# Masked graph attention on one core: forming W_v's first difference by a negation and an adding transfer, and issuing the loads of q from GpSimd

## The chip, the core and the metric

The kernel runs on one core of a Trainium2 chip. The core has five engines with queues of their own: TensorE (PE, matrix products, with its weight loads shown apart as PEld), VectorE (DVE), ScalarE (ACT), GpSimd (POOL) and SyncE (SP, which only issues transfers). Transfers between device memory and on-chip memory run on 16 DMA engines, whoever issues them. The metric is the device time of one execution in microseconds; the median of the runs counts, lower is better. The profile is one further execution, taken by the hardware profiler.

## What is computed

One layer of attention over a sparse random graph of 2708 nodes with 1024 features, all in float32:

```python
h = jnp.maximum(_layernorm(x, axis=-1), 0.0)
q = h @ W_q.T + b_q
k = h @ W_k.T + b_k
v = h @ W_v.T + b_v
z = (q @ k.T) / sqrt(1024)
z = z * adj
z = jnp.where(z == 0.0, -10000.0, z)
out = softmax(z, axis=1) @ v
x = x + jnp.maximum(out, 0.0)
```

A node has few neighbours (an entry of adj is one with probability 0.0014771), so only the scores of real neighbours matter.

## The kernel before

**Stages.** The kernel first finds the neighbours of every node, normalizes the rows to h, and sorts the nodes by their number of neighbours into tiles of 128. It folds W_q and W_k into one matrix M, so that a tile's scores are products of a row of q' = hM + b with gathered rows of h. It then runs through *units*, each a pair of tiles. Units 0 to 9 (the q units) multiply tiles of h by M and store q' rows to device memory (`q_dram` for tiles 0 to 7, `q_late` for 8 and up). Units 10 and up (the output units) multiply the attention's weighted sums u by W_v, apply the relu, add x and scatter the rows to the output. One last tile, `alone`, follows the pairs.

**Products in seven blocks.** A unit's product of a 2x2 blocked pair of tiles with a 2x2 blocked matrix is computed with seven block products instead of eight (a scheme of Strassen's kind). The matrix enters as its four blocks, held in the tile `M` (slots `M[:,0,0]`, `M[:,0,1]`, `M[:,1,0]`, `M[:,1,1]`), and as four differences, held in `T`, a view of the tile `wlow` (the name that the profile shows). Each block is 128 x 2048 in float32, 1 MB. `opened(n+1)` starts a unit during the one before it: first a11 times `M[:,0,0]`, then s1 times `T[:,0]`. `multiply` goes through the remaining five blocks and calls `after(0)` to `after(6)` between them; what a step of the neighbourhood attention or a load does "at (n, i)" is issued there.

**Change of matrix.** When the last q unit (unit 9) runs, `M` and `T` pass from the folded matrix to W_v, block by block, as TensorE finishes with them. SP loads b12, b11, b22 and b21 (line 1266; b22 twice, once into `T[:,1]`), and VectorE forms the four differences (line 1270): T0 = b12 - b11, T1 = b22 - T0, T2 = b22 - b12, T3 = b21 - T1.

**Attention beside the units.** `attention` is a stream of steps that VectorE works off between the blocks. For a tile t, `fetch` loads its q' rows into one of two buffers (`pq`, pool tag `hT`): tiles below 8 by a gather from `q_dram` issued by GpSimd, later tiles by a plain load from `q_late` issued by SP (line 833). The tile of overflow entries (`SECOND`) has half of its rows from each (line 831). `fill` gathers neighbours' rows of h into free slots (line 610, tiles `g`); there are eleven slots, and two more once `M[:,0,1]` is free for good, at (10, 1). VectorE computes the scores (line 863, gathered row times q' row), ScalarE the exponentials and the first weighted row (line 912), VectorE the sum of the rest (line 923). A slot comes free when its row has been added. Finished sums go to `u_dram`, and SP loads them back as rows `or` for the output units, by quarters for VectorE's transposes (line 705) or whole.

**Order.** VectorE's instructions stand in the order in which the program writes them. For TensorE, ScalarE, GpSimd and SP a scheduler sets the order from unit 4 on, by its own estimate of when things are ready; each engine then goes through its instructions in that order, and an instruction that waits holds up those behind it on its engine. The lines that the change touches are in `fetch` (828 to 836), `opened` (1025), `after` (1262 to 1272) and the end for `alone` (1373).

Of the kernel before, what the change touches and what calls it, by code (L numbers as in the profile page):

```python
# [14 lines left out]
AF = mybir.ActivationFunctionType  # L15
ALU = mybir.AluOpType
AX = mybir.AxisListType

P = 128
# [10 lines left out]
EARLY = 8  # L30
# [35 lines left out]
def tile_preln_masked_attention(  # L66
# [12 lines left out]
    nc = tc.nc  # L79
# [3 lines left out]
    scale = 1.0 / math.sqrt(D)  # L83
# [11 lines left out]
    HP = P // 2  # L95
# [16 lines left out]
    q_late = dram.tile([(BARE - EARLY) * P, D], FT, name="q_late")  # L112
# [63 lines left out]
    t = 0  # L176
    while t < NT:
# [4 lines left out]
        t = e  # L182
# [17 lines left out]
    M = core.tile([P, 2, 2, 4, NB], FT, name="M")  # L200
# [232 lines left out]
    T = wlow.rearrange("p (k a) (b w) -> p k (a b) w", a=2, b=2)  # L433
# [12 lines left out]
    with tc.tile_pool(name="w", bufs=1, side="left") as wp:  # L446
# [11 lines left out]
        t1 = [work.tile([P, D], FT, tag="hT", name=f"t1_{k}", bufs=2) for k in range(2)]  # L458
# [61 lines left out]
        if True:  # L520
# [13 lines left out]
            for o in range(DC):  # L534
# [4 lines left out]
                else:  # L539
                    k = o - H  # L540
# [18 lines left out]
        Z = [psum.tile([P, NB], FT, tag="acc", name=f"ps_z{i}") for i in range(H)]  # L559
# [47 lines left out]
    def gather(dst, src, t, w, n, skip=False):  # L607
        off = bass.IndirectOffsetOnAxis(ap=ptab.bitcast(U32)[:n, t, w:w + 1], axis=0)
        if skip:
            return nc.gpsimd.indirect_dma_start(out=dst, out_offset=None, in_=src, in_offset=off,  # L610
                                                bounds_check=N - 1, oob_is_err=False)
        return nc.gpsimd.indirect_dma_start(out=dst, out_offset=None, in_=src, in_offset=off)
# [176 lines left out]
    slots, free = [], []  # L789
# [13 lines left out]
    wanted, g_of, tq, first_q = [], {}, {}, []  # L803
# [11 lines left out]
    def ask(t):  # L815

        g_of[t] = []
        wanted.extend((t, s) for s in range(K[t]))

    def fetch(t):  # L820

        if t not in g_of:
            ask(t)
        if t == BARE:
            return
        assert formed.issuperset(range(EARLY) if t < EARLY or t == SECOND else (t,)), t
        tq[t] = work.tile([P, D], FT, tag="hT", name=f"pq_{t}", bufs=2)
        if t == SECOND:
            assert EARLY in formed
            gather(tq[t][:HP], q_dram[:, :], t, SLOTS - WIDE, HP)  # L830
            nc.sync.dma_start(tq[t][HP:], q_late[:HP, :])
        elif t >= EARLY:
            nc.sync.dma_start(tq[t], q_late[(t - EARLY) * P:(t - EARLY + 1) * P, :])
        else:
            got = gather(tq[t], q_dram[:, :], t, SLOTS, P)
            if t == order[0]:
                first_q.append(got)
# [171 lines left out]
    def add_block(bank, a, b, last=True):  # L1009
        for c in range(4):  # L1010
            mm = nc.tensor.matmul(bank, a[:, c, :], b[:, c, :], start=False, stop=(c == 3), skip_group_check=True)  # L1011
        return mm
# [3 lines left out]
    def opened(n):  # L1016

        if n not in banks_of:
            return
        X, Z = banks_of[n]  # L1020
        ops = ops_of[n][0]
        add_block(X, ops["a11"], M[:, 0, 0])
        Y = psum.tile([P, NB], FT, tag="acc", name="psy")
        nc.scalar.copy(Y, X)
        products.append(add_block(Z, ops["s1"], T[:, 0]))
        p5 = small("p5")
        nc.scalar.copy(p5, Z)
        opened_of[n] = Y, p5
# [158 lines left out]
    def of_wv(i, j):  # L1187

        return wv[j][:, i * 4:(i + 1) * 4, :]
# [5 lines left out]
    units = [("q",) + p for p in q_pairs] + [("o",) + p for p in o_pairs]  # L1195
# [19 lines left out]
    products = []  # L1215
    last_q = len(q_pairs) - 1
# [13 lines left out]
    for n, unit in enumerate(units):  # L1230
# [13 lines left out]
        def after(i):  # L1244
# [13 lines left out]
            if n == FIRST and i in (1, 4, 5):  # L1258
                for g in slots[:4] if i == 1 else slots[4:6] if i == 4 else slots[6:8]:
                    with tc.issue_after(sorted_at[-1].ins):  # L1260
                        nc.vector.memset(g, 0.0)
            b11, b12, b21, b22 = M[:, 0, 0], M[:, 0, 1], M[:, 1, 0], M[:, 1, 1]
            for at, place, src in (((-1, 0), b12, of_wv(0, 1)), ((0, 0), b11, of_wv(0, 0)), ((0, 2), T[:, 1], of_wv(1, 1)),
                                   ((0, 3), b21, of_wv(1, 0)), ((0, 4), b22, of_wv(1, 1))):
                if (n - last_q, i) == at:
                    nc.sync.dma_start(place, src)
            for at, place, a, b in (((0, 2), T[:, 0], b12, b11), ((0, 4), T[:, 1], T[:, 1], T[:, 0]),
                                    ((1, 0), T[:, 2], b22, b12), ((1, 1), T[:, 3], b21, T[:, 1])):
                if (n - last_q, i) == at:
                    nc.vector.tensor_sub(place, a, b)  # L1270
            if (n - last_q, i) == (1, 1):
                free.extend(M.rearrange("p i j (a c) w -> p i j a (c w)", a=2)[:, 0, 1, a, :] for a in range(2))
            if (n, i) == (FIRST, 5):
                next(stream)
            if (n, i) == (FIRST, 6):
# [39 lines left out]
            if nxt is None and i == 1:  # L1315
                uT = work.tile([P, D], FT, tag="hT", name="T_alone", bufs=2).rearrange("p (c q) -> p c q", q=P)
# [53 lines left out]
    y = work.tile([P, D], FT, tag="q", name="y_alone", bufs=4)  # L1370
    send(gather(y, x, alone, SLOTS, P))
    uT, (X, Z), p1 = single["turned"], single["banks"], single["first"]
    add_block(Z, uT[:, 0:4, :], T[:, 0])
    add_block(Z, uT[:, 4:8, :], M[:, 1, 1])
    nc.vector.tensor_add(p1, Z, p1)
    nc.vector.scalar_tensor_tensor(y[:, hi], p1, 0.0, y[:, hi], op0=ALU.max, op1=ALU.add)
# [9 lines left out]
    with tc.If(some > 0):  # L1386
# [19 lines left out]
        with tc.tile_pool(name="big", bufs=1, side="right") as big, tc.tile_pool(  # L1406
# [25 lines left out]
            for t, (t0, n) in enumerate(tiles):  # L1432
                ht = gen.tile([P, D], FT, tag="ht", name="g_h")
                nc.sync.dma_start(ht[:n], h_dram[t0:t0 + n, :])
                for s in range(DC // 4):
                    pt = psum.tile([P, 4, P], FT, tag="tp", name="g_pt")
                    for c in range(4):
                        k = s * 4 + c
                        nc.tensor.transpose(pt[:, c, :n], ht[:n, k * P:(k + 1) * P], ident[:n, :n])
                    nc.vector.tensor_copy(hT[:, s * 4:(s + 1) * 4, t0:t0 + n], pt[:, :, :n])  # L1440
            with tc.For_i(0, NT) as i:
# [9 lines left out]
                q = gen.tile([P, D + 1], FT, tag="q", name="g_q")  # L1451
# [25 lines left out]
                for b0 in range(0, N, NB):  # L1477
                    w = min(NB, N - b0)
# [84 lines left out]
```

## Time and profile before

| | |
|---|---|
| median of 3 runs | 638.18 us (637.52 to 638.37) |
| profiled execution | 638.0 us |
| its span, first to last instruction | 636.3 us |
| granted TensorE clock, mean | 0.995 |
| TensorE / VectorE / GpSimd / ScalarE busy | 98% / 83% / 57% / 45% |
| DMA | 180.11 MB, mean 283 GB/s |

The page of the profile groups instructions by line, engine and operation. A row of the timeline has the start in us from the span's start, the length in us, the engine, the line, the operation, the tiles it writes and reads, and in brackets how long its engine sat idle before it and for whom. The chain of work that ended last is followed back from the last instruction, at each step to what released it. A wait for several things is put down to the last of them. POOL rows of transfers are the time to issue them, not the transfer itself; a matmul's end is modelled.

### The profile page before, as it was taken

The numbers are of one execution on the slowest core, as the hardware profiler recorded it, in microseconds if no ns is written. First come the engines' busy times: TensorE is split into PE (matmuls) and PEld (weight loads), VectorE is DVE, ScalarE is ACT, GpSimd is POOL, SyncE is SP. The second block draws the span as 40 slices with busy tenths as digits, with TensorE's granted clock in tenths as the row PEclk, the third lists the DMA queues.
The fourth block names the chain that finished last, engine by engine and source line by source line (L and its number), as shares of the span: only waits on it lengthen the run. The fifth ranks groups of instructions, "written<-read, shape, count | busy, mean of one in ns | idle before, by whom it ended". The sixth has DMA issues, their size and how long they took to land.

```text
span 636.3 us, 6139 instructions
## 1 busy us (share of the span) xinstructions
PE 624.6 (98%) x1627; PEld 315.5 (50%) x1627; DVE 525.7 (83%) x1021; ACT 283.5 (45%) x421; POOL 361.8 (57%) x383
## 2 busy tenths in 40 slices
PE   9999999999999999999999999999999999999994
PEld 5777766444444544444444434444444444444441
DVE  5999889897995755997889999999999989898341
ACT  3539975859667533424341243443343333422300
POOL 2649960975868277563742563576566777632431
PEclk9999999999999999999999999999999999999997
DMA  8998897598696439986699998999999999893761
GB/s 339 407 372 310 334 351 298 199 342 328 246 382 221 170 113 334 326 299 196 194 289 323 297 412 216 311 318 324 351 378 321 334 299 295 242 289 95 210 217 40
DMA packets 62352, 180.11 MB, mean 283 GB/s; under 512 B 10039, under 2 KB 17031, under 8 KB 61672
## 3 DMA queue, kind: packets, MB, share of 16 engines
q0 software_dynamic: 25136, 78.41, 39.4%
q1 hardware_dynamic: 31242, 80.19, 35.8%
q10 hardware_dynamic: 5934, 21.06, 8.5%
q8 instruction: 15, 0.25, 0.2%
q14 instruction: 25, 0.20, 0.1%
HBM read 147.23 MB, written 42.31 MB: 298 GB/s over the span
## 4 chain that ended last, share of the span: by engine, by line
PE 85%; DVE 6%; issue 4%; DMA 3%; SPq 1%; POOL 0%; ACT 0%; POOLq 0%; DVEq 0%; ACTq 0%
PE ps L1011 38%; PE psy L1011 28%; PE ps_y L476 6%; PE ps_x L476 4%; PE ps_z L476 4%; PE pt L415 3%; DVE u L923 2%; DMA g<-h_dram,tab 1%; DMA or<-u_dram 1%; DVE junk L863 1%; DVE s L722 1%; DVE wlow L1270 1%; PE ps_y L511 1%; SPq L700 1%; DVE q L1092 0%
## 5 line engine op out<-in xcount | busy, mean ns | idle before, releaser
L610 POOL DMA_INDIRECT g<-h_dram,tab x94 | 121.4, 1291 | 84.4 <-DVE u L923 31.1
L1011 PE MATMUL ps<-M,a 128*128 128x512 f32 x320 | 144.0, 593 | 0.0
L1011 PE MATMUL psy<-wlow,s 128*128 128x512 f32 x320 | 143.9, 592 | 0.0
L863 DVE SCALAR_TENSOR_TENSOR junk<-g,pq 128x1024 uint8<-128x1024 f32 x93 | 113.7, 1222 | 14.0 <-DMA g<-h_dram,tab 10.9
L1011 PEld LDWEIGHTS ps<-M,a 128*128 128x128 f32 x320 | 59.8, 190 | 70.8 <-issue 70.6
L1011 PEld LDWEIGHTS psy<-wlow,s 128*128 128x128 f32 x320 | 59.7, 190 | 70.2 <-issue 69.4
L923 DVE SCALAR_TENSOR_TENSOR u<-g,coef,u 128x1024 f32<-128x1024 f32 x69 | 88.4, 1281 | 6.9 <-ACT u L912 5.8
L389 DVE FIND_INDEX8 at<-ones,adj 128x8 uint32<-128x685 f32 (+1 forms) x88 | 74.5, 865 | 0.0
L1011 PE MATMUL psy<-wlow,a 128*128 128x512 f32 x160 | 72.0, 593 | 1.4 <-DVE q L1092 1.4
L1011 PE MATMUL ps<-M,s 128*128 128x512 f32 x160 | 72.1, 592 | 0.0
L1011 PE MATMUL ps<-wlow,s 128*128 128x512 f32 x160 | 72.0, 593 | 0.1
L368 ACT ACTIVATE sized<-adj 128x2708 uint8<-128x2708 f32 (+1 forms) x22 | 54.3, 2468 | 7.5 <-DMA adj<-in_adj_dram 6.2
L298 POOL TENSOR_TENSOR hsum<-hsum,x 128x256 f32<-128x256 f32 (+1 forms) x56 | 38.7, 729 | 25.6 <-DVE wlow L444 21.2
L1110 POOL DMA_INDIRECT y<-in_x_dram,tab x19 | 34.8, 1832 | 29.1 <-ACT y L1127 15.9
L1011 PEld LDWEIGHTS psy<-wlow,a 128*128 128x128 f32 x160 | 30.3, 190 | 40.0 <-issue 37.1
L1011 PEld LDWEIGHTS ps<-wlow,s 128*128 128x128 f32 x160 | 30.3, 190 | 38.6 <-issue 37.9
L1011 PEld LDWEIGHTS ps<-M,s 128*128 128x128 f32 x160 | 30.3, 190 | 38.1 <-issue 37.4
L912 ACT ACTIVATE u<-g,coef 128x1024 f32<-128x1024 f32 x18 | 20.7, 1147 | 32.1 <-DVE coef L911 32.1
L808 POOL DMA_INDIRECT out_dram<-y,tab x21 | 25.0, 1188 | 16.4 <-DVE flag L1354 6.1
L626 POOL DMA_INDIRECT tab_dram<-tab,pos_i x22 | 21.9, 995 | 20.7 <-DVE pos_i L689 15.3
L276 ACT ACTIVATE x<-x,r 128x1024 f32<-128x1024 f32 (+1 forms) x22 | 25.9, 1235 | 7.3 <-POOL r L266 7.3
L760 ACT COPY ps<-bp_sb 128x512 f32<-128x512 f32 x42 | 24.5, 595 | 7.2 <-DVE y L1145 6.7
(251 smaller groups left out, 843.5 us busy)
## 6 DMA issues: line engine op xcount, KB each, us to landing
adj<-in_adj_dram SPq DMA_DIRECT2D x21, 1354.0 KB, 11.3
x<-in_x_dram SPq DMA_DIRECT2D x21, 512.0 KB, 3.9
h_dram<-x ACTq DMA_DIRECT2D x21, 512.0 KB, 8.7
u_dram<-v ACTq DMA_DIRECT2D x13, 512.0 KB, 6.4
or<-u_dram SPq DMA_DIRECT2D x52, 128.0 KB, 7.0
q_late<-q SPq DMA_DIRECT2D x12, 512.0 KB, 6.0
pq<-q_late SPq DMA_DIRECT2D x12, 512.0 KB, 8.6
M<-in_wv_dram SPq DMA_DIRECT2D x4, 1024.0 KB
```

The costliest lines, as they stand in the source:

```text
L276: nc.scalar.activation(xs[i][:n], xs[i][:n], AF.Relu, bias=r[:n, 4, i:i + 1], scale=r[:n, 3, i:i + 1])
L298: small.append(nc.gpsimd.tensor_add(hsum[:n, cols], hsum[:n, cols], xt[:n, cols]))
L368: nc.scalar.activation(sized[:n], a[:n, :, :PW], AF.Abs, accum_out=total[:n, t:t + 1])
L389: nc.vector.max_index(at[:n, k - first_k, g, :], ones[:n, 0:8], a[:n, g, :])
L476: mm = nc.tensor.matmul(bank, a_tile(o + H * a[0], a[1], i), b(o), start=first and o == 0, stop=(o == H - 1), skip_group_check=True)
L610: return nc.gpsimd.indirect_dma_start(out=dst, out_offset=None, in_=src, in_offset=off, bounds_check=N - 1, oob_is_err=False)
L760: nc.scalar.copy(return_[h], row[:, h * NB:(h + 1) * NB])
L808: to = nc.gpsimd.indirect_dma_start(out=out, out_offset=bass.IndirectOffsetOnAxis(ap=ptab.bitcast(U32)[:n, t, SLOTS:SLOTS + 1], axis=0), i ...
L863: chained(lambda: nc.vector.scalar_tensor_tensor(junk, g_of[t][s], 1.0, tq[t], op0=ALU.mult, op1=ALU.mult, accum_out=zall[:, t, s:s + 1]))
L923: chained(lambda: nc.vector.scalar_tensor_tensor(u, g_of[t][s], coef[:, s:s + 1], u, op0=ALU.mult, op1=ALU.add))
L1011: mm = nc.tensor.matmul(bank, a[:, c, :], b[:, c, :], start=False, stop=(c == 3), skip_group_check=True)
L1110: return nc.gpsimd.indirect_dma_start(out=y[:n], out_offset=None, in_=x, in_offset=off, compute_op=ALU.add)
```

## The change

1. T0 is no longer formed by VectorE. SP loads b11 into `M[:,0,1]` where it loaded b12, two units earlier in the program; ScalarE negates it in place in two instructions; GpSimd issues a transfer that reads b12 and adds it to what stands there. The product with s1 in the output units, and in the end for `alone`, reads `M[:,0,1]` instead of `T[:,0]`.
2. T2 is formed as T1 - b11, the same value as b22 - b12 up to rounding.
3. The two additional gather slots are the halves of `T[:,0]`, freed at (9, 0), instead of those of `M[:,0,1]` at (10, 1).
4. The loads of q' rows from `q_late` in `fetch` are issued by GpSimd instead of SP, the half tile of line 831 and the twelve whole tiles of line 833.

```diff
@@ fetch
             gather(tq[t][:HP], q_dram[:, :], t, SLOTS - WIDE, HP)
-            nc.sync.dma_start(tq[t][HP:], q_late[:HP, :])
+            nc.gpsimd.dma_start(tq[t][HP:], q_late[:HP, :])
         elif t >= EARLY:
-            nc.sync.dma_start(tq[t], q_late[(t - EARLY) * P:(t - EARLY + 1) * P, :])
+            nc.gpsimd.dma_start(tq[t], q_late[(t - EARLY) * P:(t - EARLY + 1) * P, :])
@@ opened
-        products.append(add_block(Z, ops["s1"], T[:, 0]))
+        products.append(add_block(Z, ops["s1"], T[:, 0] if units[n][0] == "q" else M[:, 0, 1]))
@@ after
-            b11, b12, b21, b22 = M[:, 0, 0], M[:, 0, 1], M[:, 1, 0], M[:, 1, 1]
-            for at, place, src in (((-1, 0), b12, of_wv(0, 1)), ((0, 0), b11, of_wv(0, 0)), ((0, 2), T[:, 1], of_wv(1, 1)),
+            b11, t1, b21, b22 = M[:, 0, 0], M[:, 0, 1], M[:, 1, 0], M[:, 1, 1]
+            for at, place, src in (((-2, 0), t1, of_wv(0, 0)), ((0, 0), b11, of_wv(0, 0)), ((0, 2), T[:, 1], of_wv(1, 1)),
                                    ((0, 3), b21, of_wv(1, 0)), ((0, 4), b22, of_wv(1, 1))):
                 if (n - last_q, i) == at:
                     nc.sync.dma_start(place, src)
-            for at, place, a, b in (((0, 2), T[:, 0], b12, b11), ((0, 4), T[:, 1], T[:, 1], T[:, 0]),
-                                    ((1, 0), T[:, 2], b22, b12), ((1, 1), T[:, 3], b21, T[:, 1])):
+            if (n - last_q, i) == (-2, 6):
+                for h in range(2):
+                    nc.scalar.activation(t1[:, 2 * h:2 * h + 2], t1[:, 2 * h:2 * h + 2], AF.Copy, scale=-1.0)
+                nc.gpsimd.dma_start(t1, of_wv(0, 1), accum_op=ALU.add)
+            for at, place, a, b in (((0, 4), T[:, 1], T[:, 1], t1), ((1, 0), T[:, 2], T[:, 1], b11),
+                                    ((1, 1), T[:, 3], b21, T[:, 1])):
                 if (n - last_q, i) == at:
                     nc.vector.tensor_sub(place, a, b)
-            if (n - last_q, i) == (1, 1):
-                free.extend(M.rearrange("p i j (a c) w -> p i j a (c w)", a=2)[:, 0, 1, a, :] for a in range(2))
+            if (n - last_q, i) == (0, 0):
+                free.extend(T.rearrange("p k (a c) w -> p k a (c w)", a=2)[:, 0, a, :] for a in range(2))
@@ the end for alone
-    add_block(Z, uT[:, 0:4, :], T[:, 0])
+    add_block(Z, uT[:, 0:4, :], M[:, 0, 1])
```

What the engines' queues look like at three places follows. On VectorE, in unit 9, the rows from the weights of a tile's sum (`u`) over the transposes and sums for the next unit's operands (`a`, `s`) to the addition that ends the unit (`q<-psy,p`, line 1092) stood like this before:

```order
L923 SCALAR_TENSOR_TENSOR u_2292<-g_1411,coef,u_2292 128x1024
L1270 TENSOR_TENSOR wlow<-M 128x2048
L923 SCALAR_TENSOR_TENSOR u_2292<-g_1412,coef,u_2292 128x1024
...
L1095 TENSOR_TENSOR q_2272<-ps_2218,u_2314 128x512
L1270 TENSOR_TENSOR wlow<-wlow 128x2048
L923 SCALAR_TENSOR_TENSOR u_2292<-g_1404,coef,u_2292 128x1024
L923 SCALAR_TENSOR_TENSOR u_2292<-g_1405,coef,u_2292 128x1024
L1092 TENSOR_TENSOR q_2273<-psy,p_2260 128x512
```

and now:

```order
L923 SCALAR_TENSOR_TENSOR u_2295<-g_1411,coef,u_2295 128x1024
L923 SCALAR_TENSOR_TENSOR u_2295<-g_1412,coef,u_2295 128x1024
...
L1095 TENSOR_TENSOR q_2275<-ps_2221,u_2317 128x512
L1274 TENSOR_TENSOR wlow<-wlow,M 128x2048
L923 SCALAR_TENSOR_TENSOR u_2295<-g_1404,coef,u_2295 128x1024
L923 SCALAR_TENSOR_TENSOR u_2295<-g_1405,coef,u_2295 128x1024
L1092 TENSOR_TENSOR q_2276<-psy,p_2263 128x512
```

One of two large subtractions ahead of the addition is gone; the other reads `M` for its second operand.

On GpSimd, in unit 5, the adding transfer (line 1270 of the changed kernel) stands between the gathers into slots and those of the rows (`qr`) for a later q unit:

```order
 L610 DMA g_1412<-h_dram,tab 128x1024
 L610 DMA g_1413<-h_dram,tab 128x1024
+L1270 DMA M<-in_wv_dram 128x2048
 L612 DMA qr_1737<-h_dram,tab 128x1024
 L612 DMA qr_1739<-h_dram,tab 128x1024
```

Nothing else moves there. ScalarE's two negations stand earlier, between its copies of lines 760 and 1076 in unit 4.

On GpSimd, in unit 6, around the q' rows of the overflow tile, stood:

```order
L612 DMA qr_1919<-h_dram,tab 128x1024
L612 DMA pq_1993<-q_dram,tab 64x1024
L610 DMA g_1411<-h_dram,tab 128x1024
L610 DMA g_1412<-h_dram,tab 128x1024
L610 DMA g_1413<-h_dram,tab 128x1024
```

and now:

```order
L612 DMA qr_1919<-h_dram,tab 128x1024
L612 DMA pq_1994<-q_dram,tab 64x1024
L610 DMA g_1411<-h_dram,tab 128x1024
L831 DMA pq_1994<-q_late 64x1024
L610 DMA g_1412<-h_dram,tab 128x1024
L610 DMA g_1413<-h_dram,tab 128x1024
```

The half load came from SP and stands between two gathers of one tile's neighbours. The twelve loads of line 833 come to stand among the later gathers in the same way, one every five to ten instructions.

## The prediction

> **What bounds the kernel now.** First the busy line of the page, then the list of what TensorE waited for, then the chain of work that ended last (columns: start, length, what).
>
> ```profile
> PE 624.6 (98%) x1627; PEld 315.5 (50%) x1627; DVE 525.7 (83%) x1021; ACT 283.5 (45%) x421; POOL 361.8 (57%) x383
> PE psy L1011 <- DVE q L1092: 1.4, 1, 1.4
> PE ps_y L511 <- POOL hsum L121: 1.2, 1, 1.2
> ```
>
> ```profile
> 283.26 0.70 DVE q L1092
> 284.10 1.11 POOL g L610
> 286.32 9.44 DMA g<-h_dram,tab
> ...
> 352.79 2.27 DVE wlow L1270
> ...
> 368.16 0.61 DVE q L1092
> 368.81 7.13 PE psy L1011 x16
> ```
>
> TensorE is busy for 624.6 of 636.3 us and waits twice: 1.2 us at the start, which the change does not touch, and 1.4 us for VectorE's addition on L1092. From 283 to 369 the chain runs over VectorE, not TensorE. So the only thing to win is what TensorE loses to VectorE near 368, and the only way to lose is to make TensorE wait somewhere new. The timeline around the wait (start, length, instruction, idle before it) shows the price:
>
> ```profile
> 352.79 2.28 DVE L1270 TENSOR_TENSOR wlow<-M 128x2048 f32<-128x2048 f32 x1
> 350.27 0.63 SPq L1266 DMA_DIRECT2D wlow<-in_wv_dram  x1
> 363.37 2.28 DVE L1270 TENSOR_TENSOR wlow<-wlow 128x2048 f32<-128x2048 f32 x1
> 363.81 3.60 PE L1011 MATMUL ps<-wlow,s 128*128 128x512 f32 x8
> 368.81 3.70 PE L1011 MATMUL psy<-wlow,a 128*128 128x512 f32 x8 [1.41 <-DVE q L1092]
> 382.65 3.60 PE L1011 MATMUL psy<-wlow,s 128*128 128x512 f32 x8
> 386.08 3.60 PE L1011 MATMUL ps<-M,a 128*128 128x512 f32 x8
> 388.90 0.69 DVE L722 TENSOR_TENSOR s<-a,s 128x512 f32<-128x512 f32 x1
> 389.74 3.67 PE L1011 MATMUL ps<-wlow,s 128*128 128x512 f32 x8
> ```
>
> and the table of busy time by stretch (stretch, its length, busy time of TensorE, weight loads, VectorE, ScalarE, GpSimd, each with its count; then clock, DMA share, GB/s) shows that VectorE had no pause there, 16.76 of 17 us:
>
> ```profile
> 352.00:369.00 17.00, 15.59 (x37) 6.65 (x36) 16.76 (x18) 2.33 (x4) 10.93 (x6) 1.00 1.05 316
> ```
>
> TensorE would have gone on at 367.40, where the block of 363.81 ends. The addition's own PSUM block had ended two blocks earlier; it came late (368.16 in the chain) because VectorE goes through its fixed order and was behind. A second, smaller loss follows: blocks start 3.43 us apart (382.65, 386.08), but the next starts 3.66 later, at 389.74, just after the operand s of 388.90: 0.23 us. Together 1.41 + 0.23 = **1.64 us is the most that a faster VectorE can return**; nothing else in TensorE's timeline up to 620 is idle.
>
> **The change, part by part.** *The subtraction b12 - b11 leaves VectorE.* It is the 2.28 us at 352.79, ahead of the addition. Between it and the addition VectorE never waits (16.76 of 17 us), so the addition moves 2.28 us earlier, unless VectorE comes to 352 late. The second subtraction (363.37) would then start at about 361.1; its 1 MB load was issued at 350.27 and had landed by 363.37. At that window's 316 GB/s, 1 MB is 3.3 us of all engines; even behind twice as much other traffic it is there at 360.2, so I take no wait (bounds 0 and 2.28 us). The other two subtractions keep their shape, place and 2.28 us.
>
> *ScalarE negates, two instructions.* They stand in this gap:
>
> ```profile
> 226.76 0.62 ACT L760 COPY ps<-bp_sb 128x512 f32<-128x512 f32 x1
> 231.69 0.59 ACT L1076 COPY taken<-psy 128x512 f32<-128x512 f32 x1 [4.31 <-PE psy L1011]
> 349.80 1.14 ACT L912 ACTIVATE u<-g,coef 128x1024 f32<-128x1024 f32 x1
> ```
>
> Two at 1.14 us (same size and engine) are 2.3 of 4.31 us of waiting for TensorE. The 1 MB they read is issued at 219.26 in SP's timeline, 8 us before them. Cost 0; without that gap it would be 2.3 us on ScalarE, whose next copy has 6.9 us (two blocks of 3.43) before TensorE wants the bank.
>
> *GpSimd issues the adding transfer of 1 MB, ahead of two row gathers.* Rows of the timeline, one of the chain (the transposes), one stretch, and two DMA issues (count, median us to landing):
>
> ```profile
> 251.92 1.29 POOL L612 DMA_INDIRECT qr<-h_dram,tab  x1 [0.30 <-issue]
> 257.94 0.94 POOL L612 DMA_INDIRECT pq<-q_dram,tab  x1 [3.46 <-DVE junk L863]
> 267.73 0.87 PE pt L415 x8
> 252.00:256.00 4.00, 4.00 (x11) 1.73 (x10) 3.52 (x10) 0.65 (x1) 2.17 (x2) 1.00 1.01 395
> 344.21 0.57 POOL L845 DMA_DIRECT2D g<-v_dram  x1 [5.24 <-DMA v_dram<-u]
> y<-in_x_dram,tab POOLq DMA_INDIRECT x21, 10.1
> g<-h_dram,tab POOLq DMA_INDIRECT x94, 7.8
> ```
>
> No row shows this form. Its issue lies between 0.57 us (a plain load, L845) and 1.29 us, plus 0.30 between issues; GpSimd waits 3.46 us soon after, which takes it in. Its bytes: 1 MB at the 395 GB/s of that window is 2.7 us of all DMA engines; an adding gather of 512 KB lands 2.3 us after a plain one (10.1 against 7.8), so 1 MB may cost 4.6 us more: 2.7 to 7.3 us, an estimate from these rows. The first gather behind it feeds the transposes at 267.73, 15.8 us after its issue; at the 8 us that gathers take here the margin is 7.8 us, against 0.9 + 2.7 to 1.6 + 7.3 us. TensorE waits 0 to 1.1 us there; I take 0, since the adding gathers of that median ran in the busiest stretches. The Trainium skill ("DMA: Bandwidth & Descriptors", Measured) has 6.15 us for a plain 1 MB load from GpSimd, inside these bounds; no run here shows one, and by that figure (an estimate: 1.6 + 6.15 of 7.8 us) TensorE waits for nothing, as in my sum.
>
> *GpSimd issues the half load of q (L831) between two gathers*; SP issued it beside them.
>
> ```profile
> 281.88 0.49 SPq L831 DMA_DIRECT2D pq<-q_late  x1
> ```
>
> The new place is on the chain: 284.10 gather, 286.32 next gather, 9.44 us to landing, which is where VectorE goes on (295.8). The insertion costs 0 (if the landing is set by bytes, which are the same) to 0.57 + 0.30 = 0.87 us of VectorE delay; I take 0.6, nearer the issue rows.
>
> *The twelve loads of q (L833) move from SP to GpSimd.* On SP their wait is the second largest (in all, times, longest):
>
> ```profile
> SPq L833 <- DVE junk L863: 72.8, 9, 18.5
> pq<-q_late SPq DMA_DIRECT2D x12, 512.0 KB, 8.6
> 393.11 1.92 POOL L610 DMA_INDIRECT g<-h_dram,tab  x1 [9.88 <-DVE u L923]
> ```
>
> Each waits for the scores of the tile whose buffer it takes, and now the gathers behind it wait too. But those need slots freed by sums that VectorE does after the same scores: at 393.11 the next gather waited 9.88 us for such a sum. So the wait mostly covers one that is there already. Each load adds 0.9 to 1.3 us to GpSimd's queue. Before 400 that falls into waits; I take 0. SP's stores and row loads, no longer queued behind these loads, come earlier, where nothing waits for them (0).
>
> The rule in the Trainium skill that speaks against the move ("DMA: Bandwidth & Descriptors", Queues, rings and completion order): each DMA engine alternates between queue rows and takes one row in ring order, so a q load gives up its own turn and stands in line with the gathers, and they behind it. The trace does not show the turns. By the rule a gather behind a q load lands 512 KB later, 1.6 us at the 335 GB/s quoted below, inside the gathers' 3 us of margin: the sum stays, and rival (2) needs less.
>
> *Two gather slots come from T's first quarter, from the last q unit on, instead of b12's place, free a unit later.* VectorE never waits for a gather between 298 and 480, so earlier gathers win nothing: 0.
>
> **Sum.** VectorE reaches the addition 2.28 - 0.6 = 1.7 us earlier, with bounds 1.4 (2.28 - 0.87) and 2.28. TensorE returns between 1.4 and 1.64; I take 1.5. The profiled execution took 638.0 us (span 636.3), 0.18 below the median 638.18; its span becomes 634.8, and the median **636.7 us**.
>
> **Rivals.** *(1) The lead is eaten before 352.*
>
> ```profile
> 261.16 1.01 POOL L610 DMA_INDIRECT g<-h_dram,tab  x1 [0.30 <-issue]
> 272.33 1.25 DVE L863 SCALAR_TENSOR_TENSOR junk<-g,pq 128x1024 uint8<-128x1024 f32 x1
> 279.82 0.69 DVE L1095 TENSOR_TENSOR q<-ps,u 128x512 f32<-128x512 f32 x1 [0.52 <-PE ps L1011]
> ```
>
> If the adding transfer costs its upper 7.3 us, gathers behind it land late too. The gather of 261.16 is used at 272.33 and takes the 7.8 us of the median, 3.4 us of margin, so VectorE could run 1 to 3 us late; at 279.82 it had 0.52 us to spare. With 1.4 us of extra delay plus 0.6, only 0.3 of the 2.28 is left and the wait of 1.41 becomes 1.1: 637.9. The 1.1 us at 267.73 points to the same place, 637.8. For it: DMA share 1.01 there. Against: margins above on every row.
>
> *(2) Slower: a q load blocks the gathers.*
>
> ```profile
> 430.00:460.00 30.00, 30.00 (x71) 13.30 (x70) 28.78 (x50) 8.73 (x16) 18.97 (x13) 1.00 1.05 335
> ```
>
> SP's loads waited 8.1 us on average (72.8 over 9). If GpSimd meets one while slots are already free, the gathers behind it start that much late and VectorE starves; VectorE is busy 28.78 of 30 us there, so it does not catch up. The margin of TensorE's operands is nothing at 389.74 and grows by about 2 us a unit. It decides from about 5 us of blocking beyond what the slots impose (3 us of gather margin, 2 of operands): one average wait, 8.1 - 5 = 3.1 us, with the 1.5 kept, gives 639.8; two give 642.9. The late variant: GpSimd issues with no pause from 493 to 519, and
>
> ```profile
> 523.78 1.22 DVE L863 SCALAR_TENSOR_TENSOR junk<-M,pq 128x1024 uint8<-128x1024 f32 x1 [1.83 <-DMA M<-h_dram,tab]
> 605.03 1.25 DVE L705 STREAM_TRANSPOSE T_alone<-or 128x1024 f32<-128x1024 f32 x1 [11.56 <-DMA or<-u_dram]
> 609.69 3.60 PE L1011 MATMUL ps<-M,T_alone 128*128 128x512 f32 x8
> ```
>
> VectorE already waits there; the last tile's transpose ends 3.4 us before TensorE needs it, and five loads at 1.3 us make 6.5, so TensorE waits 3.1 us again. Against both: the loads stand behind the gathers that need no such wait, and the 9.88 us above.
>
> *(3) The change does not reach the wait.* If VectorE's new lead only turns into waiting for the load of 350.27, TensorE keeps its 1.4 us: 638.2. It counts with (1).
>
> **How the numbers follow.** The forecast 0.45 (636.5 to 636.9), rivals (1) and (3) together 0.28 (637 to 638.3), rival (2) 0.27 (638.8 to 643). About 0.2% (1.28 us) is what a measurement can tell from no change. The forecast lies just past it, at 0.24%, and its upper edge on it: faster 0.43, within 0.30, slower 0.27. The range goes from 636.1 (all 1.64 us, and 0.4 us, half the spread of the runs shown) to 639.8, the single blocked load; it leaves out about half of rival (2).
>
> **What would show it.** The list of TensorE's waits loses the 1.4 us on L1092, and blocks around 389 start 3.43 us apart. VectorE's L1092 of that unit runs at 366 or 367 instead of 368.08. The negations stand in a gap of ScalarE before 232, and TensorE has no wait at 267. GpSimd's rows show a q load with waits for scores, followed by gathers that would have waited anyway; if instead VectorE shows new waits for gathers between 400 and 460 or above 2 us near 524, rival (2) is right. The forecast is wrong if VectorE's L863 of 295.8 starts more than 0.9 us later.

## The result, and the profile after

| | before | after |
|---|---|---|
| median of 22 runs each | 638.12 us (636.84 to 640.10) | 639.50 us (637.75 to 642.09) |
| profiled execution, its span | 638.0, 636.3 us | 641.51, 639.7 us |
| TensorE / VectorE / GpSimd / ScalarE busy | 98% / 83% / 57% / 45% | 98% / 82% / 58% / 45% |

The ratio is 1.0025 with an interval of 1.0016 to 1.0034: the change costs 1.0 to 2.2 us. The forecast was a gain of 1.5 us. The profiled execution of the changed kernel was the second longest of its 22, 2.0 us above the median.

What TensorE waited for in the changed kernel, the four largest (in all, times, longest):

```profile
PE ps L1011 <- DMA M<-in_wv_dram: 2.3, 2, 1.9
PE ps_y L511 <- POOL hsum L121: 1.2, 1, 1.2
PE pt L415 <- DMA qr<-h_dram,tab: 0.7, 1, 0.7
PE ps_in L678 <- DVE sort L666: 0.7, 1, 0.7
```

The 1.4 us for VectorE on L1092 is gone. In its place stand 2.3 us for loads of W_v's blocks b21 and b22 into `M`. The chain of waits of the same execution passes through them (start, length, what):

```profile
352.36 0.33 SPq L1266
...
352.74 9.95 DMA or<-u_dram
...
362.70 0.02 SPq L1266
...
362.75 19.43 DMA M<-in_wv_dram
...
382.31 3.67 PE ps L1011 x8
```

SP could issue the second of the two loads only when rows `or`, requested ahead of it, had landed, and the block then took 19.43 us to land. The timeline shows what else was on its way (SPq and ACTq are rows of the queues that SP and ScalarE issue from; in the chain's order of time: gathers into the new slots, T1's load, a q load, the two blocks, VectorE's addition, the waits):

```profile
346.85 1.71 POOL L610 DMA_INDIRECT wlow<-h_dram,tab  x1 [0.30 <-issue]
348.86 2.00 POOL L610 DMA_INDIRECT wlow<-h_dram,tab  x1 [0.30 <-issue]
352.16 3.60 PE L1011 MATMUL ps<-M,a 128*128 128x512 f32 x8
352.36 0.33 SPq L1266 DMA_DIRECT2D wlow<-in_wv_dram  x1
357.41 0.57 POOL L833 DMA_DIRECT2D pq<-q_late  x1 [1.02 <-DMA q_late<-q]
360.90 2.20 SPq L1266 DMA_DIRECT2D M<-in_wv_dram  x2
367.41 0.68 DVE L1092 TENSOR_TENSOR q<-psy,p 128x512 f32<-128x512 f32 x1
378.22 3.70 PE L1011 MATMUL ps<-M,a 128*128 128x512 f32 x8 [1.86 <-DMA M<-in_wv_dram]
382.31 3.67 PE L1011 MATMUL ps<-M,s 128*128 128x512 f32 x8 [0.39 <-DMA M<-in_wv_dram]
631.12 0.96 POOL L1367 DMA_INDIRECT out_dram<-y_alone,half_i  x1 [1.68 <-DVE y_alone L1383]
```

The first q load is GpSimd's at 357.41 now, ahead of the two blocks (360.90), and two gathers of 512 KB each run ahead of them too. In the kernel before, the q loads stood behind the blocks on SP, from 373.84 on. Its rows for the same stretch and for the end:

```profile
350.08 3.60 PE L1011 MATMUL ps<-M,a 128*128 128x512 f32 x8
357.23 0.92 SPq L1266 DMA_DIRECT2D M<-in_wv_dram  x2
373.84 14.16 SPq L833 DMA_DIRECT2D pq<-q_late  x3
628.24 0.97 POOL L1363 DMA_INDIRECT out_dram<-y_alone,half_i  x1 [1.67 <-DVE y_alone L1379]
```

**Where the time went.** The block `ps<-M,a` of unit 9 that uses a12 (at 350.08 before, 352.16 after) divides the span. From it to the end: 636.3 - 350.08 = 286.22 us before, 639.7 - 352.16 = 287.54 after, 1.32 more. This is 0.84 more of waiting (2.25 against 1.41 in the timeline) and 0.52 from the issue of the last scatter to the end (636.3 - 628.24 = 8.06, 639.7 - 631.12 = 8.58); the rest is the same within 0.04. Ahead of that block the profiled execution of the changed kernel is 2.08 us late. The delay is older than the first instruction that the change alters, SP's load of b11 (at 219.26 before, 221.35 after). One of TensorE's blocks ahead of that load shows it in full, before and after:

```profile
212.44 3.60 PE L1011 MATMUL psy<-wlow,a 128*128 128x512 f32 x8
214.53 3.60 PE L1011 MATMUL psy<-wlow,a 128*128 128x512 f32 x8
```

From this block to the a12 block of unit 9 it is 137.64 us before and 137.63 after, so the loads, the negations and the adding transfer in between cost TensorE nothing up to there. The same distance is 137.63 or 137.64 us in all twenty profiles of this document.

### The profile page after: what moved, and what is told of

The parts are those of the page before. It is cut to its first block, busy times and chain, and to the rows that moved or that the text cites. A ratio compares the mean times of both kernels' runs of the same rounds, so it can differ in the third digit from the quotient of the medians.

```text
span 639.7 us, 6139 instructions
## 1 busy us (share of the span) xinstructions
PE 625.0 (98%) x1627; PEld 315.2 (49%) x1627; DVE 524.4 (82%) x1020; ACT 286.9 (45%) x423; POOL 369.8 (58%) x397
## 4 chain that ended last, share of the span: by engine, by line
PE 80%; DMA 13%; DVE 4%; ACT 1%; issue 1%; POOL 0%; POOLq 0%; SPq 0%; DVEq 0%; ACTq 0%
PE ps L1011 35%; PE psy L1011 26%; PE ps_y L476 6%; DMA adj<-in_adj_dram 5%; PE ps_x L476 4%; PE ps_z L476 4%; PE pt L415 3%; DMA M<-in_wv_dram 3%; DVE at L389 2%; DMA h_dram<-x 2%; DMA or<-u_dram 2%; DMA qr<-h_dram,tab 1%; DMA wlow<-in_wq_dram 1%; DVE st L237 1%; ACT x L276 0%
## 5 line engine op out<-in xcount | busy, mean ns | idle before, releaser
L610 POOL DMA_INDIRECT g<-h_dram,tab x94 | 119.6, 1272 | 56.3 <-issue 19.2
L1011 PE MATMUL ps<-M,s 128*128 128x512 f32 x240 | 108.0, 592 | 0.4 <-DMA M<-in_wv_dram 0.4
L923 DVE SCALAR_TENSOR_TENSOR u<-g,coef,u 128x1024 f32<-128x1024 f32 x70 | 89.7, 1281 | 8.1 <-ACT u L912 6.9
L1011 PEld LDWEIGHTS ps<-M,s 128*128 128x128 f32 x240 | 45.4, 190 | 57.9 <-issue 57.2
L1110 POOL DMA_INDIRECT y<-in_x_dram,tab x19 | 33.0, 1735 | 33.3 <-ACT y L1127 16.4
L1011 PE MATMUL ps<-wlow,s 128*128 128x512 f32 x80 | 36.0, 593 | 0.0
L476 PE MATMUL ps_y<-wlow 128*128 128x512 f32 x64 | 27.6, 592 | 0.0
## 6 DMA issues: line engine op xcount, KB each, us to landing
x<-in_x_dram SPq DMA_DIRECT2D x21, 512.0 KB, 10.9
```

What stands on the lines that cost most here:

```text
L476: mm = nc.tensor.matmul(bank, a_tile(o + H * a[0], a[1], i), b(o), start=first and o == 0, stop=(o == H - 1), skip_group_check=True)
L923: chained(lambda: nc.vector.scalar_tensor_tensor(u, g_of[t][s], coef[:, s:s + 1], u, op0=ALU.mult, op1=ALU.add))
L1110: return nc.gpsimd.indirect_dma_start(out=y[:n], out_offset=None, in_=x, in_offset=off, compute_op=ALU.add)
```

## The experiments

Each kernel gave one profile and, but for four, 5 to 12 timed runs beside the kernel before. Some sets of runs scattered by 3 us and more, the kernel before too, so the profiles are compared by the table that follows them all.

**The two halves apart, the slots, and the same kernel again.** `wv_only` is the changed kernel with its loads of q back on SP; `q_only` is the kernel before with them on GpSimd. `late_slots`:

```diff
-            if (n - last_q, i) == (0, 0):
+            if (n - last_q, i) == (1, 1):
                 free.extend(T.rearrange(...
```

> Only the W_v part of the change (load of b11 into M[:,0,1], negation, adding transfer, T2 from T1, slots from T0); the loads of q stay on SP. Theory A (the moved loads of q are the cost: SP runs ahead and fills the DMA engines while the last blocks b21 and b22 of W_v are on their way): TensorE's waits for those blocks stay under 0.5 us, the 1.4 us on L1092 is gone, time 636.5 to 637.0, ratio to before about 0.998. Theory B (the two slots that come free early are the cost: two more gathers at 346 share the engines with the blocks): the waits are still there, 1.5 to 3 us, time about 639.5, ratio 1.002. Theory C (the adding transfer and its gathers cost TensorE in 200 to 270): TensorE's waits there exceed those before by 0.7 us, ratio about 1.000.

> Only the loads of q moved to GpSimd; W_v as before. Theory A: the blocks b21 and b22 arrive late for TensorE by 1.5 to 3 us and the wait on L1092 stays in some form, time 639 to 641, ratio 1.002 to 1.004. Theory B or C: no wait for these blocks, time as before, ratio 1.000.

> The changed kernel with the two additional slots (halves of T0) freed one unit and a block later, at (10, 1), as before the change. Theory A: nothing gained, ratio 1.002 to 1.003, waits for b21 and b22 still 1.5 to 3 us. Theory B: these waits go, time 637, ratio 0.998. Theory C: ratio 1.002 with the loss before 270.

> The changed kernel once more, for a second profile. If the waits for b21 and b22 belong to the kernel, TensorE waits again 1.5 to 3 us for them; if they were chance in one execution, under 0.5 us. If TensorE's loss of 0.7 us in 200 to 230 belongs to the kernel it is there again, if chance it is not. Time 639 to 640, ratio 1.0025.

Times in this set say little: ratios 1.0035 (1.0001 to 1.0069), 1.0040 (1.0008 to 1.0072), 1.0010 (0.9977 to 1.0044) and 1.0025 (0.9995 to 1.0056), with runs of the kernel before from 638.7 to 648.0 us. The timelines say more. The changed kernel again, `after_again`:

```profile
379.85 3.70 PE L1011 MATMUL ps<-M,a 128*128 128x512 f32 x8 [1.46 <-DMA M<-in_wv_dram]
384.00 3.67 PE L1011 MATMUL ps<-M,s 128*128 128x512 f32 x8 [0.45 <-DMA M<-in_wv_dram]
```

The waits for the blocks come again, 1.91 us. `q_only` has none of them and a short rest of the old wait:

```profile
357.01 0.59 POOL L833 DMA_DIRECT2D pq<-q_late  x1
369.87 3.70 PE L1011 MATMUL psy<-wlow,a 128*128 128x512 f32 x8 [0.40 <-DVE q L1092]
```

`wv_only` has no wait for the blocks and none on L1092, but VectorE now waits for the first q load, which SP issues behind the blocks at 374.5, and TensorE for VectorE:

```profile
384.63 1.22 DVE L863 SCALAR_TENSOR_TENSOR junk<-wlow,pq 128x1024 uint8<-128x1024 f32 x1 [3.58 <-DMA pq<-q_late]
392.10 3.67 PE L1011 MATMUL ps<-M,s 128*128 128x512 f32 x8 [1.51 <-DVE s L722]
```

So neither theory A nor B holds as stated: each half alone leaves the blocks on time, both together make them late. Theory C falls too: TensorE takes the same time from the block at 212 to the a12 block with the adding transfer as without. `late_slots` had 2.47 us of waits for the blocks but decides nothing on B, because the two gathers still went ahead of them: the scheduler put them at 351 and 352.4, only some 3 us later than in the changed kernel, counted from the a12 block. This kernel, which has no subtraction b12 - b11 either, also has a wait of 1.33 us on L1092: VectorE came to the addition 17.92 us after the start of the a12 block, against 15.25 and 14.40 in the two profiles of the changed kernel. Why VectorE was late there was not followed up.

**Taking each of the two early transfers away.** `no_extra` leaves the two lines that free T0's halves out; `first_q_sp`:

```diff
-            nc.gpsimd.dma_start(tq[t], q_late[...])
+            (nc.sync if t == 17 else nc.gpsimd).dma_start(tq[t], q_late[...])
```

> The changed kernel without the two additional slots (T0 stays unused after unit 9), so the two gathers near 347, 1 MB, don't run ahead of the blocks b21 and b22. Sharing theory (the blocks are late because both the early q load, 0.5 MB, and the two early gathers, 1 MB, take turns on the DMA engines; either alone is covered): TensorE's waits for the blocks fall from 1.9-2.5 us to under 0.5. Rival (the q load's 0.5 MB alone delays them): 1.5 to 2.5 us as before. Either way later gathers have fewer slots and TensorE may lose to late operands after 400; that loss is counted apart.

> The changed kernel with the first whole q load alone back on SP, where it stands behind the loads of b21 and b22 and two stores; the other eleven stay on GpSimd. Sharing theory: TensorE's waits for the blocks under 0.5 us; but VectorE waits about 3.6 us near 384 for this load, as with all loads on SP, and TensorE 1.5 us near 392. Rival (the early gathers alone delay the blocks): waits of 1.5 to 2.5 us for the blocks stay.

TensorE waited for neither block in either kernel. `no_extra` pays elsewhere, 8.8 us of TensorE's waits from 516 on: VectorE's waits for gathers rise to

```profile
DVE junk L863 <- DMA g<-h_dram,tab: 27.0, 10, 5.4
```

from 9.0 us, and the ratio is 1.0195 (1.0178 to 1.0213). By the profiles the two slots are worth some 9 us to this kernel: from the a12 block to the end it takes 296.78 us, against 287.54 with them. `first_q_sp` shows the other side of the same transfer:

```profile
383.45 1.22 DVE L863 SCALAR_TENSOR_TENSOR junk<-wlow,pq 128x1024 uint8<-128x1024 f32 x1 [4.81 <-DMA pq<-q_late]
390.91 5.37 PE L1011 MATMUL ps<-M,s 128*128 128x512 f32 x8 [2.76 <-DVE s L722]
```

More than expected (3.6 and 1.5), and the block itself runs 5.37 us where it ran 3.67; ratio 1.0096 (1.0078 to 1.0114). That is about 6 us, of which this profile shows some 3.6 (289.48 us from the a12 block to the end, 286.22 and 285.57 in the kernel before); the rest stays open. With four kernels that lack one of the two early moves and no wait for the blocks in any, and three that have both and 1.9 to 2.5 us each time, it is shown that the blocks are late because 1.5 MB go ahead of them: 0.5 MB or 1 MB alone is covered.

The bytes by queue show the exchange (GpSimd's transfers are the profile's q0, SP's its q1). The stretch is the 17 us from 1.92 us after the start of the a12 block (352.00 to 369.00 in the first profile):

| kernel | GpSimd's queue, MB | SP's queue, MB | both | waits for the blocks, us |
|---|---|---|---|---|
| before, before_again | 1.45, 1.66 | 3.90, 3.74 | 5.35, 5.40 | 0, 0 |
| q_only | 1.77 | 3.62 | 5.39 | 0 |
| first_q_sp | 2.13 | 3.41 | 5.54 | 0 |
| wv_only | 2.17 | 3.36 | 5.53 | 0 |
| no_extra | 2.34 | 3.05 | 5.39 | 0 |
| after, after_again | 2.88, 2.84 | 2.86, 2.77 | 5.74, 5.61 | 2.25, 1.91 |

The two queues together move almost the same in every kernel. What GpSimd's queue moves more, SP's, which carries the blocks, moves less. (`late_slots`, 2.13 and 3.09 MB, issues T1's load and the blocks 2 to 4 us later than the others, so the stretch isn't the same for it.)

**Issued late, or landing late?** `m_act` is the changed kernel with b21 and b22 issued by ScalarE:

```diff
-                    nc.sync.dma_start(place, src)
+                    (nc.scalar if place is b21 or place is b22 else nc.sync).dma_start(place, src)
```

> The changed kernel with the loads of b21 and b22 issued by ScalarE, not by SP. On SP both were issued only when earlier loads on that queue (T1, the rows or) had landed: b21 5.2 and 4.0 us after its place came free in the two profiles of the changed kernel, 3.5 and 2.8 in those of before. If that hold is what makes them late: b21 is issued within 1 us of its place coming free and TensorE's waits for both fall under 0.5 us. If they are late only because their bytes share the DMA engines with the early q load and gathers: waits of 1 to 2.5 us stay even though they are issued earlier.

```profile
353.25 3.60 PE L1011 MATMUL ps<-M,a 128*128 128x512 f32 x8
353.45 0.64 SPq L1266 DMA_DIRECT2D wlow<-in_wv_dram  x1
356.89 0.34 ACTq L1266 DMA_DIRECT2D M<-in_wv_dram  x1
367.25 2.29 DVE L1274 TENSOR_TENSOR wlow<-wlow,M 128x2048 f32<-128x2048 f32 x1 [2.72 <-DMA wlow<-in_wv_dram]
372.72 3.70 PE L1011 MATMUL psy<-wlow,a 128*128 128x512 f32 x8 [2.13 <-DVE q L1092]
```

b21 is issued the moment its place is free (353.25 + 3.60 = 356.85), and TensorE waits for neither block. But now T1's load, issued at 353.45, has landed only at 367.25, 13.8 us later (in the changed kernel VectorE read it 10.3 us after its issue without a wait), VectorE's addition is late, and the old wait is back with 2.13 us. I read this as: the hold on SP's queue decided which transfer came late, and the bytes in the window that one did. It rests on one execution, and that was the slowest of this kernel's twelve (642.42 us, median 639.84). Ratio 0.9988 (0.9970 to 1.0006), not told from no change.

Both parts add to the delay in the changed kernel. There the two blocks were issued 8.7 and 10.6 us after the start of the a12 block and took 17.3 and 19.4 us to land; in `no_extra` they were issued 6.8 and 7.6 us after it and took 14.0 and 17.5. `first_q_sp` issued them as late as `after_again` (8.0 and 10.2 against 7.6 and 9.7), yet TensorE didn't wait.

**One block out of the window.** T0's place is free from unit 9's start. `b21_early` loads b21 there and takes the two slots from `M[:,1,0]`:

```diff
-            b11, t1, b21, b22 = M[:, 0, 0], M[:, 0, 1], M[:, 1, 0], M[:, 1, 1]
+            b11, t1, b21, b22 = M[:, 0, 0], M[:, 0, 1], T[:, 0], M[:, 1, 1]
-                                   ((0, 3), b21, of_wv(1, 0)), ...
+                                   ((0, 0), b21, of_wv(1, 0)), ...
-            if (n - last_q, i) == (0, 0):
-                free.extend(T.rearrange("p k (a c) w -> p k a (c w)", a=2)[:, 0, a, :] for a in range(2))
+            if (n - last_q, i) == (0, 3):
+                free.extend(M.rearrange("p i j (a c) w -> p i j a (c w)", a=2)[:, 1, 0, a, :] for a in range(2))
-        add_block(X, ops["a12"], M[:, 1, 0])
+        add_block(X, ops["a12"], M[:, 1, 0] if units[n][0] == "q" else T[:, 0])
-    add_block(X, uT[:, 4:8, :], M[:, 1, 0])
+    add_block(X, uT[:, 4:8, :], T[:, 0])
```

> The changed kernel with b21 loaded into T0's place, which is free from unit 9's start, about 17 us earlier than its old place; the additional slots are the halves of M[:,1,0] instead, free from (9, 3). If the late landing of the two blocks is what the changed kernel lost: no wait for them over 0.4 us, none of 1.4 us on L1092 either, and TensorE idle under 1 us between 230 and 620 (2.25 and 1.91 in the changed kernel, 1.64 before); time 1.5 to 2 us below the changed kernel, ratio to before 0.998 to 1.000. If the loss lies elsewhere (the end of the kernel, the issue of loads by GpSimd): ratio 1.002.

> The kernel before once more, for a second profile: the ratio should be 1.000, its TensorE should wait about 1.4 us on L1092 again. The wait of 0.7 to 2.4 us for a row gather near 203, seen in every profile but that of before, is chance if it shows here, and so is the longer time from the last scatter to the end (8.6 to 8.8 us with the loads of q on GpSimd, 8.1 and 8.2 without) if it is over 8.5 here.

> b21_early once more: its 12 runs had a median like that of before with some at 640 to 644. If these belong to the kernel they come again; if chance, the ratio is 0.997 to 0.999. TensorE again without a wait between 230 and 620.

> A third profile of b21_early. If the scatter of its executions comes from loads of q that block gathers: in a slow one (640 us or more) from the a12 block of unit 9 to the end over 286 us, with waits of VectorE for gathers or of TensorE for operands after 390. If it lies ahead of 350: 284.8 to 285.2 us there, as in the first two profiles, and the a12 block later than 351.

> A fourth profile of b21_early, read as the third: over 286 us from the a12 block to the end if blocked gathers make the slow executions, 284.8 to 285.2 us if the scatter lies ahead of 350.

In three of its four profiles TensorE has no wait at all after 230, in the fourth 0.44 us for b22. Yet its time was 1.0013 (0.9991 to 1.0036) and 1.0023 (0.9997 to 1.0050) of the kernel before, with single runs of up to 644.3 and 647.9 us. The second profile, of 641.03 us, lost its time ahead of the a12 block: that block starts at 354.13, against 350.14 in the third (637.04 us), and from there to the end both take 285.2 us. No longer execution of this kernel was profiled, so where those lose their time stays open.

The kernel before, again, shows what one profile is worth. Its TensorE waits:

```profile
PE ps_y L511 <- POOL hsum L121: 1.2, 1, 1.2
PE ps L1011 <- DVE s L722: 0.7, 1, 0.7
```

The wait of 1.4 us on L1092, on which the prediction rests, isn't there in this execution; 0.66 us for s at 389 is. VectorE came to the addition 16.51 us after the start of the a12 block, against 18.00 in the first profile.

**The loads of q, with b21 out of the way.** `b21_sp` is `b21_early` with all loads of q on SP, `b21_mix` with the first four whole ones on GpSimd and the rest on SP; `q_first7` and `q_last5` are the kernel before with that many of the twelve on GpSimd.

> As b21_early, with all loads of q back on SP. If the 0.5 us between last scatter and end come from the loads on GpSimd: 8.1 to 8.2 us there, not 8.6. VectorE waits again for the first q load near 384 (3.6 us with wv_only; less here, since b21 is no longer ahead of it); TensorE loses 0 to 1.5 us near 392 by it. Ratio to before 0.997 without that wait, 1.000 with it.

> As b21_early, but only the first four whole loads of q on GpSimd; the half load and the last eight on SP. If the 0.5 us at the end come from any load on GpSimd: 8.6 us; if they grow with their number: 8.2 to 8.4. TensorE without a wait between 230 and 620; ratio 0.997 to 0.999.

> The kernel before with the first seven of the twelve whole loads of q issued by GpSimd. If the longer end is set by the number of loads that GpSimd issues: 8.3 to 8.5 us from last scatter to end. If by loads issued late in the program: 8.1 to 8.2.

> The kernel before with the last five of the twelve whole loads of q issued by GpSimd. By number: 8.2 to 8.4 us from last scatter to end; by lateness: 8.6 to 8.8.

> b21_sp once more. Its first profile had no wait of TensorE after 230 and 284.3 us from the a12 block of unit 9 to the end, against 286.2 and 285.6 in two profiles of the kernel before. If that holds in most executions: ratio to before 0.997 to 0.998. If the executions that were timed have waits which the one profile did not show: 0.999 to 1.001.

> b21_mix once more: 284.4 us from the a12 block of unit 9 to the end in its first profile. Ratio to before 0.997 to 0.998 if that holds, 0.999 to 1.001 if not; 0.1 us more than b21_sp at the end.

In the first set the ratios were 0.9986 (0.9969 to 1.0004) and 0.9988 (0.9972 to 1.0004), in the second 0.9981 (0.9972 to 0.9991) and 0.9991 (0.9981 to 1.0000). So in the second set `b21_sp` beats the kernel before, with a median of 636.56 us beside 637.87; in the first the interval reaches 1. The changed kernel was not run beside it, but its own ratio was 1.0025. SP's timeline in the second execution shows how:

```profile
343.65 0.33 SPq L1266 DMA_DIRECT2D wlow<-in_wv_dram  x1
350.52 0.33 SPq L1266 DMA_DIRECT2D wlow<-in_wv_dram  x1
359.00 0.35 SPq L1266 DMA_DIRECT2D M<-in_wv_dram  x1
364.42 0.32 SPq L833 DMA_DIRECT2D pq<-q_late  x1
```

b21 goes at 343.65; behind b22 at 359.00 the q load goes at 364.42. Counted from the a12 block (350.32 here, 352.66 in `wv_only`) that is 7.7 us earlier than in `wv_only`. VectorE still waits 1.65 us for it (line 863, at 380.34), against 3.58 there, and not at all in the first profile of `b21_sp`; TensorE has no wait after 230 in either profile.

The table takes each profile apart: the start of the a12 block of unit 9, from there to the end of the span, and of that TensorE's waits, the time from the issue of the last scatter to the end, and what remains.

| kernel, loads of q on GpSimd | a12 block at | to the end | waits | last scatter to end | remains |
|---|---|---|---|---|---|
| before, 0 | 350.08 | 286.22 | 1.41 | 8.06 | 276.75 |
| before_again, 0 | 350.43 | 285.57 | 0.66 | 8.10 | 276.81 |
| after, 13 | 352.16 | 287.54 | 2.25 | 8.58 | 276.71 |
| after_again, 13 | 354.19 | 287.41 | 1.91 | 8.80 | 276.70 |
| late_slots, 13 | 352.97 | 289.33 | 3.80 | 8.56 | 276.97 |
| q_only, 13 | 352.15 | 285.85 | 0.40 | 8.68 | 276.77 |
| wv_only, 0 | 352.66 | 286.14 | 1.51 | 8.19 | 276.44 |
| first_q_sp, 12 | 350.22 | 289.48 | 2.76 | 8.58 | 278.14 |
| no_extra, 13 | 350.42 | 296.78 | 8.83 | 8.55 | 279.40 |
| m_act, 13 | 353.25 | 287.45 | 2.13 | 8.85 | 276.47 |
| b21_early (four), 13 | 350.14 to 354.13 | 284.80 to 285.43 | 0 to 0.44 | 8.55 to 8.96 | 276.19 to 276.44 |
| b21_mix (two), 4 | 353.48, 350.82 | 284.42, 284.68 | 0 | 8.22, 8.48 | 276.20 |
| b21_sp (two), 0 | 354.80, 350.32 | 284.30, 284.38 | 0 | 8.10, 8.18 | 276.20 |
| q_first7, 7 | 350.94 | 286.36 | 1.20 | 8.39 | 276.77 |
| q_last5, 5 | 350.30 | 286.40 | 1.10 | 8.64 | 276.66 |

The start of the a12 block scatters from 350 to 355 with the set of runs, not with the kernel: 350.1 to 351.0 in the sets of `before_again`, `b21_sp_again` and `b21_early_p3`, with and without the change, 352 and later in the two others, `q_only` among them, which has the instructions of the kernel before up to 281. In the late ones TensorE waits up to 2.4 us for a row gather near 203. With the constant 137.63 us behind that, the whole scatter lies ahead of 213, in instructions that all these kernels share: the 2.08 us in the first profile aren't the change's. Why one set is late and another isn't stays open.

## Why the prediction was wrong

- *The wait for VectorE's addition goes when the subtraction goes: right in both profiles of the changed kernel.* The addition ran at 367.41, which is 2.75 us earlier than before when both are counted from the a12 block; TensorE had no wait for it, and T1's subtraction found its load there, as taken. The wait can come back when VectorE or T1's load is late, as `late_slots` (1.33 us) and `m_act` (2.13 us) show. *Its size, 1.64 us, was that of one execution.* Five profiles with W_v formed as before wait 1.41, 0.66, 0.40, 1.20 and 1.10 us (the second and the last for s near 389, the others on L1092). The mean of 0.95 is a third less than 1.41.
- *The negations and the adding transfer, taken at 0: right.* No wait of TensorE stands at the transposes behind them, and from the block at 212.44 to the a12 block TensorE takes 137.63 us with them as without. The transfer's issue took 1.03 us, inside its bounds. Rival (1) falls with this: in the changed kernel VectorE had its lead at the addition.
- *The half load between two gathers, taken at 0.6 us of VectorE: not seen.* VectorE waited 1.24 + 2.14 = 3.38 us for the two gathers there, 3.10 + 0.94 = 4.04 before.
- *"The twelve loads of q: 0", "SP's stores and row loads come earlier, where nothing waits for them (0)" and "earlier gathers win nothing: 0": this is the step that failed.* Each was priced by its issue and by who waits for it, and that part was right. What was left out is what a transfer that comes earlier goes ahead of. The first q load moved from 373.84 to 357.41, from behind b21 and b22 to ahead of them; the two gathers into T0's halves moved from 377 to 347. TensorE then waits 1.9 to 2.5 us for the blocks. The prediction's table of stretches had the warning: between 352 and 369 the DMA share was 1.05. In this window there was no spare transfer time: what GpSimd's queue moved more, SP's moved less. Every move of bytes forward is then a move of other bytes back, and no term of the sum could be 0 without naming those. The rule on queue rows that the prediction cited (the Trainium skill, "DMA: Bandwidth & Descriptors", Queues, rings and completion order) was weighed for the gathers behind a q load alone; the waits above are those of SP's ring, which by that rule gives turns to GpSimd's. The traces agree in direction, with GpSimd's queue moving 2.88 MB in the 17 us of the table in place of 1.45, and SP's 2.86 in place of 3.90; they don't show the turns.
- *The end of the kernel was no step at all.* The prediction took a new wait of TensorE for the only way to lose. From the last scatter to the end, the eleven profiles with 12 or 13 loads of q on GpSimd take 8.68 us on the average, the five without any 8.13: 0.55 us that TensorE has no part in.
- *Rival (2) had the sign and not the place.* VectorE's waits for gathers fell (9.0 us against 10.9), none stands between 400 and 460, and T_alone is waited for as long as before (11.7 us). Rival (3), a wait for T1's load, came true in `m_act` alone.

By the two profiles of each, the changed kernel pays 2.08 - 1.04 = 1.04 us in waits and 8.69 - 8.08 = 0.61 us at the end, less 0.07 in what remains: 1.58 us, against 1.38 between the medians. So the waits for the blocks, 2.08 us, take what the old wait gave back, 1.04 us, and as much again. The end, measured and not explained, adds the rest. What the greater scatter of kernels with the loads on GpSimd adds to that stays open.

## What to carry to other kernels

Where the DMA share is at 1 (1.05 in this stretch), ask of every transfer that a change lets go earlier which transfer it now precedes, and who waits for that one; a price of 0 needs that answer, not only the answer that nobody waits for the transfer itself. TensorE's wait for a late transfer went here when bytes left the stretch (b21 15 us earlier, counted from the a12 block, into a place that was free); another queue made the next transfer late. And a wait of 1.4 us in one profile is a draw: a second profile of the kernel before showed 0.7, in another place. A point that all profiles share, as the block at 212.44 here, tells what a change did from what the execution brought along.

## What the runs showed of the hardware

- A load's issue can hang on the landing of another one on its queue. SP's waits in the changed kernel between 350 and 366:

```profile
SPq L1266 <- DMA wlow<-in_wv_dram: 3.2, 1, 3.2
SPq L1266 <- DMA or<-u_dram: 1.4, 1, 1.4
```

  b21 was issued at 360.90, though its place was free at 352.16 + 3.60 = 355.76. Before the change the same waits were 2.4 and 0.2 us. Issued by ScalarE (`m_act`), it went as soon as its place was free. What makes SP wait isn't shown.
- In that stretch 1 MB took 17.3 and 19.4 us to land, where its bytes at 316 GB/s would be 3.3 us of all engines (an estimate).
- In the 17 us of the table by queue, GpSimd's and SP's queues together moved 5.35 to 5.74 MB in eight profiles, while GpSimd's part went from 1.45 to 2.88 MB.
- An adding transfer of 1 MB took GpSimd 1.03 us to issue.
- The end: 8.06 to 8.19 us from the last scatter's issue in five profiles without loads of q on GpSimd, 8.55 to 8.96 in eleven with 12 or 13. Neither their number nor their being late explains it cleanly: four gave 8.22 and 8.48, the first seven 8.39, the last five 8.64. The cause is open.
